# Chained sums of four selective scans on TensorE, a deferred C product on GpSimd and a later product of silu

## The chip, the cores and the metric

The kernel runs on one core of one Trainium2 chip. The metric is the device time of one execution in microseconds (us), as the median of several executions. One execution is profiled; its trace gives the views that are quoted here. The engines are called PE (TensorE's products), PEld (its weight loads), DVE (VectorE), ACT (ScalarE), POOL (GpSimd) and SP (the sync engine, which issues nearly all DMAs here).

## The reference, cut to what matters

The model is a convolution and gated selective scan block, followed by an attention and a feed-forward block on the same tokens. The scan runs over 4 batches, 4 directions, 192 channels, 16 states and 4096 positions. The part that the change touches is this:

```python
xconv = jax.nn.silu(t)                                   # t: the convolution's output
x_flat = xconv.reshape(Bn, Dn, L)                        # rows of the image
x_tr = xconv.transpose(0, 1, 3, 2).reshape(Bn, Dn, L)    # columns of the image
...                                                      # directions 0, 1; 2, 3 are these reversed
def step(h, inp):
    ut, dt, Bt, Ct = inp
    dA = jnp.exp(dt[..., None] * A[None])
    h = dA * h + (dt * ut)[..., None] * Bt[:, :, None, :]
    y = jnp.einsum('bkdn,bkn->bkd', h, Ct)
    return (h, y)
...
return y + D[None, :, :, None] * u
...
inv_y = jnp.flip(out_y[:, 2:4], axis=-1)
y = out_y[:, 0] + inv_y[:, 0] + wh_y + invwh_y           # wh_y, invwh_y: turned back to rows
mu = jnp.mean(y, axis=-1, keepdims=True)                 # a layer norm follows
```

## The kernel before

A scan is cut into 1536 pieces of 128 partitions (32 channels by 4 states) by 1024 positions: 4 batches, 4 directions in the order 1, 3, 0, 2, 4 stretches of positions, 6 groups of 32 channels, 4 sets of states. Here is the loop over pieces. `back` is a generator for all other work: the convolution of later batches, the turn of the column scans and the epilogue (layer norm, attention, feed-forward) of finished ones; the loop takes one step of it per piece.

```python
for i in range(n):
    self.at = i
    self.loads(i)                      # dl: delta and delta*u; bc: B and C rows
    if i >= 1:
        self.carry(i - 1)              # ACT, a small copy
    if i + 1 < n:
        self.decay(i + 1)              # ACT: dA = exp(dl * A)
    full = i % 8 == 3 and i > 8
    if full:
        self.evacuate(i - 4)           # ACT: ys <- yp, then stored
    elif i >= 3:
        self.reduce(i - 3)             # PE: sum over states into yp
    if i + AHEAD < n:
        self.inject(i + AHEAD)         # POOL: w = dl * B
    self.scan(i)                       # DVE: h = scan(dA, w); then w = h * C
    c.later.tick()
    ...                                # prepares delta of later pieces
    next(back, None)
    if full:
        self.reduce(i - 3)
```

The product with C goes to GpSimd or VectorE, as a static tally of their work decides, and the reduce sums over 4 sets of states in PSUM:

```python
c.vec.tensor_tensor_scan(h, dA, w, first, ALU.mult, ALU.add)
(c.gps if pool else c.vec).tensor_tensor(w, h, cr, ALU.mult)
...
for x in range(4):                     # reduce
    c.nc.tensor.matmul(
        y[32 * x : 32 * x + 32, g % 2, :], c.sum4, prod[:, 256 * x : 256 * x + 256],
        start=(q == 0), stop=(q == NQ - 1), tile_position=(0, 32 * x),
    )
```

Each direction's output `yd[k]` goes to DRAM. The turn adds directions 1 and 3 on TensorE and copies the sum in transposed order; the layer norm adds the rest, also on TensorE:

```python
for i, t in enumerate(ts):             # turn: yd[1] and yd[3]
    nc.tensor.matmul(ps, c.i96, t, start=(i == 0), stop=(i == 1))
yield
nc.scalar.copy(
    yh.rearrange("p (h w) -> p h w", w=IW)[:, :, 8 * q : 8 * q + 8],
    ps.rearrange("p (w h) -> p h w", h=IH),
)
...
for h in range(2):                     # the epilogue's layer norm
    ps = bank(f"ys{h}", h)[0:96]
    mm(ps, [(c.i96, x["y0"][:, h]), (c.i96, x["y2"][:, h]), (c.i96, x["y13"][:, h]), (c.dskip[:, h], x["u"][:, h])])
    yield
    t = f32(f"ysum{h}")
    nc.scalar.copy(t, ps)
```

silu and the sign of its input, one step (`yield`) of `back` after the other:

```python
elif s == 1:
    sg = f32("sg" + pn)[0:96, 0:128]
    nc.scalar.activation(
        sg.bitcast(F8).rearrange("p (h e i) -> p h i e", h=8, e=2),
        pz.rearrange("p (h i e) -> p h i e", h=8, e=2), AF.Sign, saturate=False,
    )
    ...
    nc.scalar.activation(e, pz, AF.Exp, scale=-1.0)
else:
    nc.scalar.activation(e, e, AF.Ln, bias=1.0)
    nc.scalar.activation(e, e, AF.Exp, scale=-1.0)
    u = f32("u" + pn)[0:96]
    c.vec.tensor_tensor(u, pz, e, ALU.mult)
```

## Time and profile before

The median is 5782.8 us over 4 executions. The profiled execution spans 5775.5 us. I cut every profile at two points of VectorE's timeline, the start of its first scan and the end of its last one:

| part | us | what sets it |
|---|---|---|
| start, to the first scan | 287.9 | loads, the convolution of batch 0, its silu |
| scans | 5321.9 | VectorE works 5026.5 of it, GpSimd 5023.6 |
| tail, after the last scan | 165.8 | last layer norm, attention, feed-forward |

VectorE thus idles 295.4 us of the middle part. The prediction below shows the lines behind this. It mentions ScalarE's waits without showing them; here they are, from the waits of ScalarE in the kernel before (what waited and its line, what it waited for, then us in total, how often, and the longest):

```profile
ACT ysum L889 <- PE ys L836: 138.9, 52, 11.0
ACT yh L746 <- PE tn L744: 44.6, 18, 10.6
```

Both instructions stand at the head of ScalarE's queue while TensorE waits for a load, and the decays stand behind them. In the kernel before, the evacuation `ys <- yp` never does this for long. Its line (count, busy us and mean ns, idle time just before and what ended it) shows 8.6 us of waiting for TensorE in all:

```profile
L1276 ACT COPY ys<-yp 128x512 f32<-128x512 f32 x192 | 111.8, 582 | 8.6 <-PE yp L1264 8.6
```

### The profile page before, as it was taken

What the parts mean: (1) busy time and instruction counts of PE and PEld (TensorE: products, weight loads), DVE (VectorE), ACT (ScalarE), POOL (GpSimd) and SP (SyncE); (2) the same over time, 40 slices, a digit from 0 to 9 for tenths busy, and PEclk for the clock granted to TensorE, in tenths of its full rate; (3) what the DMA queues carried; (4) which work ended last, traced back from release to release, by engine and by line L of the source; (5) the groups of instructions that cost most, each with busy time, mean ns of one, the idle gap of its engine ahead of it and who ended that gap; (6) DMA issues with size and microseconds to landing.
All of it is one profiled execution on the core that took longest, in us unless ns stands there. A gap on an engine that the chain in (4) does not pass through costs nothing. (4 is left out here: it accounts for less than half of the span.)

```text
span 5775.5 us, 61921 instructions
## 1 busy us (share of the span) xinstructions
PE 3419.4 (59%) x19813; PEld 1339.9 (23%) x19813; DVE 5176.7 (90%) x3422; ACT 3672.1 (64%) x5620; POOL 5080.7 (88%) x2291
## 2 busy tenths in 40 slices
PE   6446645664468755666446875563477654353577
PEld 3222222222223322222212322221122211111123
DVE  3299999999889999999999999999999999999984
ACT  5567876886556566788655656755556676554544
POOL 2099999999889999999998999999999999999980
PEclk8666755676678866666567885565688765565687
DMA  4455656655676655665567665575667555575652
GB/s 75 105 169 189 196 180 200 194 170 178 200 222 213 205 177 176 204 189 164 184 218 226 209 206 177 182 223 190 207 195 214 191 189 185 174 222 180 197 160 73
DMA packets 589452, 1069.91 MB, mean 185 GB/s; under 512 B 225867, under 2 KB 295556, under 8 KB 587332
## 3 DMA queue, kind: packets, MB, share of 16 engines
q1 hardware_dynamic: 575636, 1065.88, 59.3%
q8 instruction: 156, 2.56, 0.2%
q10 hardware_dynamic: 13488, 0.07, 0.1%
q14 instruction: 172, 1.41, 0.1%
HBM read 833.20 MB, written 229.38 MB: 184 GB/s over the span
## 5 line engine op out<-in xcount | busy, mean ns | idle before, releaser
L386 POOL TENSOR_TENSOR w<-dl,bc 128x1024 f32<-128x1024 f32 x1536 | 3578.4, 2354 | 149.2 <-PE yp L1264 73.8
L1223 ACT ACTIVATE dA<-dl,anm 128x1024 f32<-128x1024 f32 x1536 | 1714.0, 1116 | 494.6 <-DVE w L386 254.6
L1264 PE MATMUL yp<-w,sum 128*32 128x256 f32 x12288 | 1323.3, 547 | 845.8 <-ACT ys L1276 447.7
L386 DVE TENSOR_TENSOR_SCAN dA<-dA,cy,w 128x1024 f32<-128x1024 f32 x680 | 1593.1, 2343 | 109.7 <-ACT dA L1223 94.0
L386 POOL TENSOR_TENSOR w<-h,bc 128x1024 f32<-128x1024 f32 x631 | 1483.8, 2352 | 191.6 <-DVE h L386 181.0
L386 DVE TENSOR_TENSOR w<-dA,bc 128x1024 f32<-128x1024 f32 x905 | 1108.6, 1225 | 57.9 <-DVE dA L386 0.9
L386 DVE TENSOR_TENSOR_SCAN h<-dA,cy,w 128x1024 f32<-128x1024 f32 x472 | 1103.8, 2340 | 12.0 <-ACT dA L1223 10.2
L1264 PEld LDWEIGHTS yp<-w,sum 128*32 128x32 f32 x12288 | 363.1, 137 | 1941.0 <-issue 836.8
L386 DVE TENSOR_TENSOR_SCAN dA<-dA,w 128x1024 f32<-128x1024 f32 x225 | 513.6, 2283 | 38.3 <-ACT dA L1223 29.9
L1254 ACT COPY cy<-dA 128x1 f32<-128x1 f32 x680 | 105.8, 156 | 666.2 <-DVE w L386 665.7
L562 PE MATMUL cv<-tp,cw 96*96 96x512 fp8e5 x1152 | 390.8, 499 | 137.5 <-ACT r L611 110.0
L386 DVE TENSOR_TENSOR_SCAN h<-dA,w 128x1024 f32<-128x1024 f32 x159 | 362.3, 2279 | 32.0 <-POOL w L386 23.7
L562 PEld LDWEIGHTS <-cw 96*96 96x96 fp8e5 x1152 | 174.3, 158 | 358.2 <-issue 314.6
L744 PE MATMUL tn<-yt,ident 96*96 96x512 f32 x256 | 175.1, 820 | 111.8 <-DMA yt<-yd 111.1
L836 PE MATMUL ys<-ey,ident 96*96 96x512 f32 x336 | 184.7, 692 | 75.2 <-DMA ey<-yd 47.4
L1254 ACT COPY cy<-h 128x1 f32<-128x1 f32 x472 | 87.6, 186 | 193.5 <-DVE h L386 193.5
L575 ACT ACTIVATE sg<-cz 96x512 fp8e5<-96x512 f32 x64 | 159.0, 2484 | 22.1 <-DVE cz L386 22.0
L1166 ACT ACTIVATE pd<-dps,dbias,pvd 128x512 f32<-128x512 f32 x189 | 143.7, 760 | 23.1 <-PE dps L1161 23.1
L386 DVE TENSOR_TENSOR u<-cz,e 96x512 f32<-96x512 f32 x64 | 43.8, 684 | 115.6 <-ACT e L586 108.6
L1167 ACT ACTIVATE sp<-dps,dbias,pvd 128x512 f32<-128x512 f32 x189 | 144.6, 765 | 0.0
L836 PE MATMUL fc<-x,mean 96*96 96x512 f32 x54 | 51.9, 1064 | 151.9 <-DVE x L386 151.9
L386 DVE TENSOR_TENSOR pd<-dps,pu 128x512 f32<-128x512 f32 x189 | 130.7, 691 | 8.6 <-DMA pu<-ud 2.2
(305 smaller groups left out, 4448.1 us busy)
## 6 DMA issues: line engine op xcount, KB each, us to landing
dl<-dld SPq DMA_DIRECT2D x768, 512.0 KB
bc<-bcd SPq DMA_DIRECT2D x512, 512.0 KB
dld<-pd SPq DMA_DIRECT2D x126, 512.0 KB
yd<-ys SPq DMA_DIRECT2D x768, 64.0 KB
dld<-pd SPq DMA_DIRECT2D x126, 256.0 KB
yt<-yd SPq DMA_DIRECT2D x128, 192.0 KB
ey<-yd SPq DMA_DIRECT2D x58, 384.0 KB
pu<-ud SPq DMA_DIRECT2D x32, 512.0 KB
```

Source lines behind the costliest of these rows:

```text
L386: return getattr(self.eng, name)(out, *args, **kw)
L562: nc.tensor.matmul(ps, c.cw[:, j, t, 96 * h : 96 * h + 96], tpad[j][:, 8 * q + dy : 8 * q + dy + 8, dx : dx + IW], start=(j == 0 and t == ...
L575: nc.scalar.activation(sg.bitcast(F8).rearrange("p (h e i) -> p h i e", h=8, e=2), pz.rearrange("p (h i e) -> p h i e", h=8, e=2), AF.Sign ...
L744: nc.tensor.matmul(ps, c.i96, t, start=(i == 0), stop=(i == 1))
L836: self.c.nc.tensor.matmul(ps, w, x, start=(i == 0), stop=(i == len(pairs) - 1))
L1166: nc.scalar.activation(d[:, 0], ps, AF.Abs, scale=sc, bias=bi)
L1167: nc.scalar.activation(t, ps, AF.Relu, scale=sc, bias=bi)
L1223: c.nc.scalar.activation(t, self.dlt[i // NQ][0], AF.Exp, scale=c.anm[:, g, NQ * KORD[e] + q : NQ * KORD[e] + q + 1])
L1254: self.c.nc.scalar.copy(self.carries[g, q], h[:, CH - 1 : CH])
L1264: c.nc.tensor.matmul(y[32 * x : 32 * x + 32, g % 2, :], c.sum4, prod[:, 256 * x : 256 * x + 256], start=(q == 0), stop=(q == NQ - 1), tile ...
```

## The change

The intent is to take those two waits, and the TensorE and VectorE work of the sums, away. Scan 3 adds the output of scan 1 while it reduces, scan 2 adds that of scan 0, the turned sum, and D times u; the outputs are loaded into a new tile `ya` and multiplied into the PSUM tile of the reduce. Besides, the product with C on GpSimd is queued behind the next inject, sg is written in a row, silu's product comes a step later (and the taps of the convolution are spread over four steps instead of three), the turn goes ahead of the next convolution, the evacuation goes ahead of the decay, an output counts as settled after 8 pieces instead of 16, and in the last 64 pieces the work behind takes two steps per piece. The diff, cut to its core:

```diff
-                for s in range(3):
+                for s in range(4):
...
-                                sg.bitcast(F8).rearrange("p (h e i) -> p h i e", h=8, e=2),
-                                pz.rearrange("p (h i e) -> p h i e", h=8, e=2), AF.Sign, saturate=False,
+                                sg.bitcast(F8).rearrange("p (h e i) -> p h e i", h=8, e=2),
+                                pz.rearrange("p (h i e) -> p h e i", h=8, e=2), AF.Sign, saturate=False,
...
-                        else:
+                        elif s == 2:
                             nc.scalar.activation(e, e, AF.Ln, bias=1.0)
                             nc.scalar.activation(e, e, AF.Exp, scale=-1.0)
+                        else:
                             u = f32("u" + pn)[0:96]
                             c.vec.tensor_tensor(u, pz, e, ALU.mult)
... (turn: no products on TensorE, yh copied straight from the loaded yd[3])
... (layer norm: no ys products and no ysum copies; it loads the finished sum)
-        (c.gps if pool else c.vec).tensor_tensor(w, h, cr, ALU.mult)
+        if pool:
+            self.late = (w, h, cr)
+        else:
+            c.vec.tensor_tensor(w, h, cr, ALU.mult)
...
+    def load_sums(self, i):
+        b, e, ci, g, q = self.pieces[i]
+        k = KORD[e]
+        if k < 2:
+            return
+        at = CH * (NCH - 1 - ci)
+        t = c.p.ya.tile([128, 3, 256], F32, name=f"ya_{i}", tag="ya")          # one buffer
+        whole = lambda d: d.rearrange("h p l -> (h p) l")
+        srcs = [c.yd[1][b]] if k == 3 else [c.yd[0][b], whole(c.y13[b]), whole(c.ud[b])]
+        for j, src in enumerate(srcs):
+            c.nc.sync.dma_start(
+                t[:, j], src[32 * g : 32 * g + 32, at : at + CH].rearrange("d (x l) -> x d l", x=4)
+            )
+        self.sums[i // NQ] = [(t[:, j, ::-1], c.dskip[:, g] if j == 2 else c.back4) for j in range(len(srcs))]
... (reduce, on the last of the four sets of states)
+        for n, (src, w) in enumerate(more):
+            c.nc.tensor.matmul(y[:, g % 2, :], w, src, start=False, stop=(n == len(more) - 1))
... (the loop over pieces)
             self.loads(i)
+            if i % NQ == NQ - 1:
+                while KORD[self.pieces[i][1]] == 2 and self.pieces[i][0] not in c.turned:
+                    next(back)
+                self.load_sums(i)
             if i >= 1:
                 self.carry(i - 1)
+            if i % 8 == 3 and i > 8:
+                self.evacuate(i - 4)
             if i + 1 < n:
                 self.decay(i + 1)
-            full = i % 8 == 3 and i > 8
-            if full:
-                self.evacuate(i - 4)
-            elif i >= 3:
+            if i >= 3:
                 self.reduce(i - 3)
             if i + AHEAD < n:
                 self.inject(i + AHEAD)
+            self.late_product()
             self.scan(i)
...
             next(back, None)
-            if full:
-                self.reduce(i - 3)
+            if i > n - 64:
+                next(back, None)
```

## The prediction

> **What bounds the kernel now.** I read the page first, then the waits of VectorE and GpSimd alone, then busy time by stage, then the chain at the end. The kernel runs 1536 pieces of a selective scan (128x1024). Each needs one GpSimd product w<-dl,bc (the inject), one VectorE scan, and one product with C on either engine, which a static tally decides.
>
> ```profile
> PE 3419.4 (59%) x19813; PEld 1339.9 (23%) x19813; DVE 5176.7 (90%) x3422; ACT 3672.1 (64%) x5620; POOL 5080.7 (88%) x2291
> ...
> L386 POOL TENSOR_TENSOR w<-dl,bc 128x1024 f32<-128x1024 f32 x1536 | 3578.4, 2354 | 149.2 <-PE yp L1264 73.8
> ...
> L386 POOL TENSOR_TENSOR w<-h,bc 128x1024 f32<-128x1024 f32 x631 | 1483.8, 2352 | 191.6 <-DVE h L386 181.0
> L386 DVE TENSOR_TENSOR w<-dA,bc 128x1024 f32<-128x1024 f32 x905 | 1108.6, 1225 | 57.9 <-DVE dA L386 0.9
> ...
> L744 PE MATMUL tn<-yt,ident 96*96 96x512 f32 x256 | 175.1, 820 | 111.8 <-DMA yt<-yd 111.1
> L836 PE MATMUL ys<-ey,ident 96*96 96x512 f32 x336 | 184.7, 692 | 75.2 <-DMA ey<-yd 47.4
> ...
> L575 ACT ACTIVATE sg<-cz 96x512 fp8e5<-96x512 f32 x64 | 159.0, 2484 | 22.1 <-DVE cz L386 22.0
> ```
>
> Two engines are near full and nothing else is. The timeline puts the first scan at 287.85 us and the last work of the scans at about 5613. Busy time in that stretch, then in one batch's layer-norm sums, then in a stretch with hardly any work behind the scans (columns: window, length, then busy us of PE, weight loads, DVE, ACT, POOL, then clock, DMA share, GB/s):
>
> ```profile
> 287.85:5613.00 5325.15, 3159.54 (x18774) 1204.50 (x18773) 5027.10 (x3152) 3456.04 (x5310) 5026.74 (x2180) 0.67 0.61 193
> ```
> ```profile
> 1660.00:1990.00 330.00, 253.85 (x1236) 94.71 (x1234) 300.25 (x199) 195.23 (x318) 300.37 (x131) 0.82 0.69 213
> ```
> ```profile
> 5130.00:5450.00 320.00, 126.96 (x909) 42.11 (x906) 311.33 (x185) 165.52 (x252) 313.32 (x136) 0.56 0.59 190
> ```
>
> So the span is 288 us of start, 5325 of scans and 163 of tail. In the scans both engines work 5027 us: the 298 us of idle time is all that a change of waits can win there. The quiet stretch idles 2.7%, the sums 9%. What ends the idle time in the scans (VectorE, then GpSimd):
>
> ```profile
> DVE dA L386 <- ACT dA L1223: 123.9, 82, 8.5
> DVE u L386 <- ACT e L586: 44.3, 28, 3.4
> DVE h L386 <- POOL w L386: 24.0, 3, 16.8
> ```
> ```profile
> POOL w L386 <- DVE h L386: 181.0, 174, 6.0
> POOL w L386 <- PE yp L1264: 74.3, 33, 5.9
> ```
>
> VectorE waits for ScalarE's decay dA although ScalarE is only 64% busy: a decay stands in ScalarE's queue behind something that itself waits. ScalarE's own waits name it: ysum for PE's ys 138.9 us, yh for PE's tn 44.6 us. In the tail the chain goes through loads:
>
> ```profile
> 5619.26 9.52 DMA ln1b<-yd
> 5628.87 10.94 DMA eu<-ud
> 5639.91 0.81 DVE ey L386 x2
> 5641.97 3.73 PE mu L836 x4
> ```
>
> **What the Trainium skill says.** "TensorE: Matmul & The Clock Gate", section "Architectural detail: the array is 16× 32×32, not 1× 128×128", calls ScalarE, VectorE and GpSimd strict FIFOs. The trace agrees: with a third of ScalarE's time free, decays still came up to 8.5 us late. "SBUF — State Buffer", section "Door 1: The DMA port swizzle", says that consecutive accesses to one 16-byte line of SBUF run at full bandwidth and each change of line costs. The trace agrees for writes: sg writes bytes 32 apart and takes 2484 ns, while xsT, as many fp8 elements written in a row, takes 672. It agrees for reads: the ut copy reads SBUF at a 256-byte step and takes 1100 ns, while yh makes the same kind of transposition out of PSUM in 575. "DMA: Bandwidth & Descriptors", section "Anatomy of one DMA — SWDGE (gpsimd) path", says a DMA's semaphore wait happens on the issuing sequencer. Here the sync queue waited 891.8 us for decays before reloading dl, so a new load placed behind a dl load also waits.
>
> **The change, part by part.**
>
> *Chained sums.* The four directional outputs are now added inside the reduce's PSUM accumulation: scan 3 adds scan 1's output; scan 2 adds scan 0's, the turned sum, and D times u. Removed from TensorE: tn 175.1 us; ys 184.7; the D product in ys and the bias product in sy, 112 passes each like ys (184.7/336 = 0.55 us), 2 x 62; 484 us in all. Added: 96 + 288 = 384 products of 256 columns in two passes, 768 x 0.275 = 211 us. Net about -270 us, off the path. What counts is that ScalarE loses 56 ysum copies (32.5 us) with their 139 us of waits, and yh no longer waits for TensorE. yh now reads SBUF at a step, so it should cost about 1.1 us like ut: 64 x 0.52 = +34 us. Traffic is a draw: 64 x 192 KB + 96 x 384 KB leave, 384 x 128 KB come, both 50.3 MB, now in 1 KB runs instead of 2 KB.
>
> *sg written in a row.* 2484 to about 700 ns: 64 x 1.78 = -114 us of ScalarE. In the start, 16 of these lie on the chain cz, sg, e, e, e, u, v, r. One part takes 7.4 us there; without 1.8 it would take 5.6, where TensorE, busy 15 of each 20 us, also nears its limit (7.4 x 0.75 = 5.6). I take 6.0: 16 x 1.4 = **-22 us** at the start.
>
> *silu's product a step later.* u no longer stands at VectorE's head while its exponential runs: most of 44 us in the scans. In the start nothing else stands there, so no gain.
>
> *C product behind the next inject.* A GpSimd product now has one inject (2.35 us) more before it needs h. The 174 waits average 1.04 us, so most vanish as seen from GpSimd. But both engines idle the same 298 us, and GpSimd's waits are largely VectorE's lateness passed on; I count this as slack, not as a second sum.
>
> *Order and depth.* The evacuation goes ahead of the decay, the settling distance falls from 16 to 8 pieces, the turn precedes the prologue, and the work behind gets two steps per piece in the last 64 pieces. The instruction order shows no pile-up: at most 7 ScalarE instructions between two decays in both kernels. It also shows 6 instead of 4 of the last batch's eight columns done under the scans.
>
> *Sum in the scans*, by stage, with idle time (length minus VectorE's busy time, my cut of the timeline): turn and sums 1609 us, 129 idle (8.0%), to 4%: -65. Convolution 645, 50 idle (7.8%), to 4%: -25. The remaining 3070, 119 idle (3.9%), to 3.3%: -19. Against that +8 for two more columns of epilogue and +7 for waits on the added loads. **-94 us**.
>
> *Tail.* Before, mu of the last lane starts at 5642 behind 3 x 6 loads and the adds. Now two columns in two lanes need three loads each and no adds, so mu can start near 5622, and lane 0 has no second round (5672 to 5697). From mu to the end of kv took 29 us, so the middle part starts near 5653 instead of 5697: **-44 us**. The 78 us after it stay.
>
> Sum: 5783 - 22 - 94 - 44 = 5623; I say 5620.
>
> **Rivals.**
> (a) The added loads become the wait. They have one buffer, queue behind 1 MB of dl loads, and the last of them is needed by an evacuation that now stands ahead of a decay. For: DMA is already 69% busy in the sums. Against: some four pieces (14 us) lie between issue and use, and a 1.4 MB burst at the 310 GB/s seen at the start needs 4.5 us. If each of 96 loaded PSUM tiles cost 1.5 us: 5620 + 144, about 5765.
> (b) The idle time merely moves: VectorE waits for other things at ScalarE's head (fq, xq, sq wait 117 us for TensorE), or GpSimd for w buffers, because products come later. Then only start and tail count: about 5715.
> (c) The slack works everywhere and all stages reach the quiet stretch's 2.7%: 5027/0.973 = 5167, -158 in place of -94: about 5560.
>
> **Range and chances.** Start and tail are the surer 66 us; 2% is 116 us, so the scans must give 50 of their 298. (c) is as near as (b), and (a) is what would undo it. Range 5535 to 5700. Faster by over 2%: 0.78; within 2%: 0.19; slower: 0.03.
>
> **What would show it.** sg near 700 ns and yh near 1100; first scan near 266 us; u <- e gone in the scans; dA <- ACT dA from 124 to about 50; w <- h from 181 to under 60; the stretch between start and tail near 5230; tail near 119. Wrong if yp waits for the new loads by more than about 50 us and decays wait behind ys, or if POOL w <- PE yp grows beyond its 74.

## The result, and the profile after

The changed kernel takes 5711.7 us (median of 4, 5707.2 to 5716.4) against 5782.8. A ratio here is the mean time of one kernel's fast runs over that of the other's of the same rounds, so it is not quite the ratio of the medians: it is 0.988, with a 95% interval of 0.9863 to 0.9897. That is within 2%, where the prediction expected more than 2%, and above its range, which ended at 5700.

| part | before | after | change | predicted |
|---|---|---|---|---|
| start | 287.9 | 264.7 | -23.1 | -22 |
| scans | 5321.9 | 5326.6 | +4.7 | -94 |
| tail | 165.8 | 119.2 | -46.6 | -44 |

Start and tail came as worked out. The whole miss is in the scans, which gave nothing. First the page of the changed kernel: the engines' busy time, then groups (line, engine, operation and shapes, count, busy us and mean ns, idle time just before and what ended most of it):

```profile
PE 3355.5 (59%) x19813; PEld 1348.7 (24%) x19813; DVE 5157.6 (90%) x3396; ACT 3566.1 (62%) x5564; POOL 5075.9 (89%) x2295
...
L401 POOL TENSOR_TENSOR w<-h,bc 128x1024 f32<-128x1024 f32 x633 | 1490.4, 2355 | 127.7 <-DVE h L401 121.5
...
L1294 PE MATMUL yp<-ya,back 128*128 128x256 f32 x576 | 286.0, 607 | 253.9 <-DMA ya<-yd 222.7
...
L1303 ACT COPY ys<-yp 128x512 f32<-128x512 f32 x192 | 112.2, 585 | 122.9 <-PE yp L1294 112.7
```

The tn and ys products are gone, and ScalarE has 106 us less to do (3672.1 before). But the last two lines look like the old trouble again: the new products waited 222.7 us for the load of an earlier output, and the evacuation, idle for 8.6 us before, now waits 112.7 us for those products. The same stretch as the prediction's first window, from the first scan to the last (columns as there):

```profile
264.73:5591.30 5326.57, 3127.62 (x18796) 1225.91 (x18795) 5028.31 (x3161) 3392.30 (x5278) 5029.13 (x2187) 0.65 0.61 195
```

VectorE (the third number after the length) and GpSimd (the fifth) have the same work as before, in a stretch of the same length. So hardly any work was added on the bounding engines: VectorE's idle time is 298.3 us where it was 295.4. The waits of VectorE, GpSimd and TensorE in the changed kernel say what ends it now:

```profile
DVE dA L401 <- ACT dA L1221: 122.8, 70, 10.0
...
DVE u L401 <- ACT e L601: 39.8, 16, 2.5
DVE h L401 <- ACT dA L1221: 30.5, 14, 7.6
```
```profile
POOL w L401 <- DVE h L401: 121.5, 106, 4.2
...
POOL w L401 <- PE yp L1289: 74.3, 43, 6.3
```
```profile
PE yp L1294 <- DMA ya<-yd: 222.7, 78, 9.8
...
PE yp L1294 <- DMA ya<-y: 31.1, 47, 1.7
...
PE yp L1294 <- DMA ya<-ud: 26.0, 52, 1.2
```

VectorE waits for late decays 122.8 + 30.5 = 153.3 us; before it was 123.9 + 17.9 = 141.8. The prediction put the late decays down to ysum and yh; those waits are gone, and the decays are as late as before, so something else holds them now. The 39.8 us of u lie in the start, where u has nothing else to run beside. TensorE waited 222.7 + 31.1 + 26.0 = 279.8 us for the added loads.

One such event, from the changed kernel's timeline (start, length, queue or engine, operation, and in brackets the wait just before it):

```profile
1306.92 6.18 SPq L1198 DMA_DIRECT2D dl<-dld  x2
...
1313.20 0.57 SPq L1275 DMA_DIRECT2D ya<-yd  x1
...
1314.42 0.69 SPq L1275 DMA_DIRECT2D ya<-ud  x1
...
1319.61 1.22 PE L1294 MATMUL yp<-ya,back 128*128 128x256 f32 x2 [4.11 <-DMA ya<-yd]
...
1324.05 1.22 PE L1294 MATMUL yp<-ya,dskip 128*128 128x256 f32 x2 [0.88 <-DMA ya<-ud]
...
1325.30 0.58 ACT L1303 COPY ys<-yp 128x512 f32<-128x512 f32 x1 [3.68 <-PE yp L1294]
...
1325.79 1.12 ACT L1221 ACTIVATE dA<-dl,anm 128x1024 f32<-128x1024 f32 x1
...
1327.01 2.30 DVE L401 TENSOR_TENSOR_SCAN dA<-dA,w 128x1024 f32<-128x1024 f32 x1 [3.13 <-ACT dA L1221]
```

The sync queue is held 6.18 us by the two dl loads ahead (the next two, at 1325.70, take it 1.22 us; in between it waited until 1311.84 for a decay, which frees their buffer), so the first ya load leaves at 1313.20. It is used 6.4 us later, and the third one, issued at 1314.42, 9.6 us later. TensorE was ready for the first at 1319.61 - 4.11 = 1315.50, only 2.3 us after its issue. The evacuation needs all three and stands in front of the decay; the decay stands in front of the scan. VectorE loses 3.13 us. It is one event; the hold of the queue is longer than in most.

ScalarE's groups by shape show the sizes that were predicted for single instructions:

```profile
L755 ACT COPY yh<-yt 96x512 f32<-96x512 f32 x64 | 68.9, 1076 | 13.5 <-DMA yt<-yd 12.9 <-ACT sp L1165 0.5
...
L590 ACT ACTIVATE sg<-cz 96x512 fp8e5<-96x512 f32 x64 | 37.6, 588 | 25.6 <-DVE cz L401 25.4
L598 ACT ACTIVATE e<-cz 96x512 f32<-96x512 f32 x64 | 37.3, 584 | 0.0
```

sg takes 588 ns where it took 2484, now the same as its neighbour e; the prediction said 700. That e, whose own patterns did not change, took 936 ns before. yh takes 1076, as predicted. In the chain that ended last, the tail's first links are shorter than before, but the new loads head it:

```profile
5591.21 5.65 DMA ya<-ud
...
5600.93 3.62 DMA eys<-yd
5604.69 3.70 PE mu L848 x4
```

mu starts 5604.69 - 5591.30 = 13.4 us after the last scan. Before, it started 5641.97 - 5609.73 = 32.2 us after it: one load now brings a finished sum where four loads and three additions stood. From mu to the middle part (where the prediction has 5697) it was 5697.08 - 5641.97 = 55.1 us, and now 5631.82 - 5604.69 = 27.1: the second round of lane 0 is gone.

Last, the scans by direction, in the order in which they run, summed over the four batches. I counted the scan instructions of VectorE's timeline and took the starts of every 96th:

| us | scan 1 | scan 3 | scan 0 | scan 2 | last 64 pieces (in scan 2) |
|---|---|---|---|---|---|
| before | 1362 | 1308 | 1328 | 1324 | 217 |
| after | 1327 | 1309 | 1286 | 1405 | 252 |

So the change does win in the scans, 35 us in scan 1 and 42 us in scan 0. It loses 81 us in scan 2, where each PSUM tile waits for six loads (three for each of its two groups), and some 35 of these are in the last 64 pieces.

### The profile page after: what moved, and what is told of

Its sections match the earlier page's. It is cut to its first block, busy times and chain, and to the rows that moved or that the text cites.

```text
span 5710.5 us, 61945 instructions
## 1 busy us (share of the span) xinstructions
PE 3355.5 (59%) x19813; PEld 1348.7 (24%) x19813; DVE 5157.6 (90%) x3396; ACT 3566.1 (62%) x5564; POOL 5075.9 (89%) x2295
## 5 line engine op out<-in xcount | busy, mean ns | idle before, releaser
L401 POOL TENSOR_TENSOR w<-dl,bc 128x1024 f32<-128x1024 f32 x1536 | 3581.3, 2358 | 151.7 <-PE yp L1289 74.3
L1289 PE MATMUL yp<-w,sum 128*32 128x256 f32 x12288 | 1363.2, 551 | 1009.6 <-POOL w L401 580.4
L401 POOL TENSOR_TENSOR w<-h,bc 128x1024 f32<-128x1024 f32 x633 | 1490.4, 2355 | 127.7 <-DVE h L401 121.5
L401 DVE TENSOR_TENSOR_SCAN h<-dA,cy,w 128x1024 f32<-128x1024 f32 x474 | 1108.0, 2339 | 30.5 <-ACT dA L1221 30.5
L1289 PEld LDWEIGHTS yp<-w,sum 128*32 128x32 f32 x12288 | 342.4, 136 | 2080.9 <-POOL w L401 882.2
L1294 PE MATMUL yp<-ya,back 128*128 128x256 f32 x576 | 286.0, 607 | 253.9 <-DMA ya<-yd 222.7
L1294 PEld LDWEIGHTS yp<-ya,back 128*128 128x128 f32 x576 | 131.0, 274 | 423.4 <-DMA ya<-yd 281.4
L577 PEld LDWEIGHTS <-cw 96*96 96x96 fp8e5 x1152 | 161.7, 151 | 283.1 <-issue 237.0
L1303 ACT COPY ys<-yp 128x512 f32<-128x512 f32 x192 | 112.2, 585 | 122.9 <-PE yp L1294 112.7
L848 PE MATMUL yc<-eys,mean 96*96 96x512 f32 x240 | 130.5, 695 | 21.7 <-DMA esz<-szd 7.6
L401 DVE TENSOR_TENSOR dps<-dps,sp 128x512 f32<-128x512 f32 x189 | 129.1, 683 | 0.0
```

What stands on the lines that cost most here:

```text
L401: return getattr(self.eng, name)(out, *args, **kw)
L577: nc.tensor.matmul(ps, c.cw[:, j, t, 96 * h : 96 * h + 96], tpad[j][:, 8 * q + dy : 8 * q + dy + 8, dx : dx + IW], start=(j == 0 and t == ...
L848: self.c.nc.tensor.matmul(ps, w, x, start=(i == 0), stop=(i == len(pairs) - 1))
L1289: c.nc.tensor.matmul(y[32 * x : 32 * x + 32, g % 2, :], c.sum4, prod[:, 256 * x : 256 * x + 256], start=(q == 0), stop=(q == NQ - 1 and no ...
L1294: c.nc.tensor.matmul(y[:, g % 2, :], w, src, start=False, stop=(n == len(more) - 1))
L1303: c.nc.scalar.copy(t, y[:, :, ::-1] if k >= 2 else y)
```

## The experiments

My theory after the result was that the loads of ya arrive late, and pass the delay on through TensorE, the evacuation and the decay. The rivals: the place of the evacuation ahead of the decay is the cost, whatever it waits for; the added products or the added traffic slow TensorE or the DMA engines as such; the deferred C product turns GpSimd's idle time into waits for buffers. A second round asked about the doubled steps of the last 64 pieces, and whether the small parts gave what was predicted of them. All 15 kernels ran with three timed rounds; ratios are against the kernel before in the same rounds. In the tables, "scans" is always the stretch from the first scan to the end of the last, in one profile each; four executions of one kernel differ by 8 to 23 us in all (5707.2 to 5716.4 above), and the rounds ran on different chips, so a difference of some 15 us between two profiles means nothing alone.

### Without the chained sums (result wrong)

```diff
-            if i % NQ == NQ - 1:
-                while KORD[self.pieces[i][1]] == 2 and self.pieces[i][0] not in c.turned:
-                    next(back)
-                self.load_sums(i)
```

> The changed kernel without the chained loads and their products in the reduce (a wrong result on purpose: the epilogue gets scan 2's output alone); all else as in the changed kernel, 5712 us. Scans 0, 1, 2, 3 of the four batches took 331+..., in sum 1284 us (scan 0), 1327 (scan 1), 1400 (scan 2), 1312 (scan 3) there. Theory A (the gain of the removed waits is given back because loads and products of the chain hold the evacuation, and with it the decay, in scan 2): scan 2 falls from 1400 to about 1310 us, VectorE's wait for decays from 153 to under 70, time about 5620. Theory B (the loss in scan 2 comes from the doubled steps at the end and from the work that moved there, not from the chain): at most 20 us less, about 5695.

Measured: 5633.6 us, ratio 0.9758 (0.9741 to 0.9774), scans 5250.3. The output is wrong, with a relative error of 0.158, as it must be. Loads, added products and the wait for the turn are all gone; the scans get 76 us shorter. The cost is in the chained sums; which part of them, this run can't say. (The sums by direction in the expectation are off by up to 5 us from the table above.)

### The added products without their loads (result wrong)

```diff
-        t = c.p.ya.tile([128, 3, 256], F32, name=f"ya_{i}", tag="ya")
+        t = self.still                       # a resident tile of zeros
...
-        for j, src in enumerate(srcs):
-            c.nc.sync.dma_start(
-                t[:, j], src[32 * g : 32 * g + 32, at : at + CH].rearrange("d (x l) -> x d l", x=4)
-            )
```

> The chain's 384 products stay but read a tile that is resident (a wrong result on purpose), so only the 384 loads go. Theory A1 (it is the late loads that hold the evacuation): as without the chain, about 5625. Theory A2 (it is TensorE's 286 us of added products): about as the changed kernel, 5700 or more.

Measured: 5639.9 us, ratio 0.9772 (0.9758 to 0.9787), scans 5259.0; wrong by the same 0.158. TensorE still does every added product here, and only some 9 us of the scans come back against the run above. So the products themselves cost too little to tell from the noise, and 5326.6 - 5259.0 = 67.6 us are due to the loads (by the ratios, about 62). That can be their lateness or their traffic.

### The evacuation behind the decay again

```diff
-            if i % 8 == 3 and i > 8:
-                self.evacuate(i - 4)
             if i + 1 < n:
                 self.decay(i + 1)
+            if i % 8 == 3 and i > 8:
+                self.evacuate(i - 4)
```

> Only the evacuation goes back behind the decay of the next piece, as in the kernel before. Theory A with the evacuation ahead of the decay as the culprit: one decay is shielded from its wait, a decay later still has to wait behind it, and the 112.7 us that ScalarE waits there for yp fall on VectorE by about a piece (3.4 us) less each in 44 cases: about 5660. If the order of the two doesn't matter (the evacuation still stands ahead of the decay after it): 5705 to 5715.

Measured: 5686.8 us, ratio 0.9854 (0.984 to 0.9869), scans 5297.3, result correct. VectorE's wait for dA falls from 122.8 to 79.7 us. By the ratios the place is worth 0.0026 of the time, about 15 us, with intervals that just overlap, and by the scans 29; the time lies between the two forecasts. It is a place in which a late evacuation does more harm; it isn't what makes it late.

### The loads one piece earlier, ahead of the dl loads

```diff
-            if i % NQ == NQ - 1:
-                while ...
-                self.load_sums(i)
...
                 self.reduce(i - 3)
+            if i % NQ == 2:
+                while ...
+                self.load_sums(i + 1)
```

> The chain's loads are issued one piece earlier, right behind the reduce that frees their buffer and so ahead of the 1 MB of dl loads of the next piece instead of behind them. If the loads are late because they queue behind the dl loads and the decay that these wait for (theory A1): TensorE's wait for ya falls from 280 us to under 100 and the time to about 5650. If the sync queue then waits for TensorE in their place (it waited 85 us already for yp there): no gain, 5700 or more.

Measured: 5714.1 us, ratio 0.9897 (0.9879 to 0.9915), scans 5325.2, correct: no gain. The sign of theory A1 came, but not its time: TensorE's wait for ya fell from 279.8 to 53.4 us and VectorE's for dA from 122.8 to 92.5. The waits of the sync queue show where the gain went:

```profile
SPq L1275 <- PE yp L1294: 468.7, 96, 14.6
```

There is one buffer of ya. Issued this early, the load must wait until TensorE has read the buffer's last contents, and it waits at the head of the one queue that carries all loads. In the changed kernel this wait is 84.8 us. The loads behind it then come late: GpSimd waited 36.0 us for bc, against 2.7, and VectorE 12.6 us for bc and 21.5 for x1b, against 4.7 and 13.4. So an earlier load alone moves the wait from TensorE to the sync queue; it needs a free buffer too.

### Two loads for each group, in two buffers, three pieces earlier

A second buffer of three rows did not fit in SBUF when I built it. This version moves D times u to scan 3, in the turned order of u, so that scans 3 and 2 load two rows each. Bytes and number of loads stay: 96 x 2 + 96 x 2 instead of 96 x 1 + 96 x 3.

```diff
-ya=pool("yap", 1)
+ya=pool("yap", 2)
...
-        t = c.p.ya.tile([128, 3, 256], F32, name=f"ya_{i}", tag="ya")
+        t = c.p.ya.tile([128, 2, 256], F32, name=f"ya_{i}", tag="ya")
-        srcs = [c.yd[1][b]] if k == 3 else [c.yd[0][b], whole(c.y13[b]), whole(c.ud[b])]
+        srcs = [c.yd[1][b], whole(c.utd[b])] if k == 3 else [c.yd[0][b], whole(c.y13[b])]
-        self.sums[i // NQ] = [(t[:, j, ::-1], c.dskip[:, g] if j == 2 else c.back4) for j in range(len(srcs))]
+        self.sums[i // NQ] = [(t[:, j, ::-1], c.dskip[:, g] if (k, j) == (3, 1) else c.back4) for j in range(len(srcs))]
...
-            if i % NQ == NQ - 1:
+            if i % NQ == 0:
```

> The chain is kept and correct, but its loads get time: D times u joins in scan 3 (from the turned u) instead of scan 2, so that each of the two scans has two loads, the buffer shrinks from three to two rows of 256 and is doubled, and the loads are issued three pieces earlier, ahead of the dl loads, into a buffer free since the group before the last. Number of loads and bytes as in the changed kernel (ratio 0.988 to before). Theory A1 (only their lateness costs): the ratio of the run without loads, 0.977, and TensorE's wait for ya under 60 us. If the traffic or the sync queue's time costs, not the lateness: 0.985 to 0.988.

Measured: 5648.7 us, ratio 0.9781 (0.9757 to 0.9805), scans 5265.7, correct. Whether it is over 2% faster than the kernel before stays open. VectorE's wait for the decays before dA, 122.8 us in the changed kernel, is down by a third (before h, from 30.5 to 26.7):

```profile
DVE dA L401 <- ACT dA L1221: 80.4, 58, 8.5
```

TensorE no longer waits for ya at all. I paired each load of an earlier output with the first product that uses it. In the changed kernel TensorE waited for 78 of these 192 loads; in the median of these it stood ready 5.0 us after the issue, and the product began 7.5 us after it. In this run the median from issue to use is 21 us. With the same bytes, the scans are 60.9 us shorter, 90% of the 67.6 us that taking the loads away had given (by the ratios, 57 of 62). So it was mainly the lateness, not the traffic. The second buffer, the earlier issue and the even split of the loads were not tested one by one.

### The same with the evacuation behind the decay

The edit is that of the third experiment on top of the fifth.

> The same with the evacuation behind the decay as in the kernel before. If with timely loads the evacuation no longer waits, its place is worth nothing more: within 0.002 of the run with two loads each. If it still waits for the products (TensorE in order behind other work), 0.003 less.

Measured: 5646.7 us, ratio 0.977 (0.9744 to 0.9795), scans 5265.7, correct. It can't be told from the run above (0.9781). Once the loads are in time, no effect of the evacuation's place is seen.

### The C product in its old place

```diff
-        if pool:
-            self.late = (w, h, cr)
-        else:
-            c.vec.tensor_tensor(w, h, cr, ALU.mult)
+        (c.gps if pool else c.vec).tensor_tensor(w, h, cr, ALU.mult)
```

> The changed kernel with GpSimd's C product back at its place before the next inject. If the deferral hides the wait for h (the prediction's slack): GpSimd's w <- h wait goes from 121 back to about 180 us and the time grows by 20 to 40 us, ratio 0.992 to 0.995. If GpSimd's wait was VectorE's lateness passed on: within 0.002 of 0.988. If the deferral makes the reduces late and so costs: 0.984.

Measured: 5709.0 us, ratio 0.9879 (0.9854 to 0.9903), scans 5325.2, correct. The time is that of the changed kernel (0.988), but GpSimd's waits are not: 208.0 us for h instead of 121.5, and 12.0 + 6.2 for yp instead of 74.3.

### The kernel before with the deferred C product, sg in a row and silu's later product

The edit takes these three parts of the diff above, and nothing else, into the kernel before.

> The kernel before with the deferred C product, the sign written in a row and silu's product a step later, without the chained sums, the new order of the work behind and the doubled steps. The start must gain its 23 us. If the scans' waits in convolution and quiet pieces are won by these three alone: 45 us more, ratio about 0.988. If their scan part is small and the gain in scans 0 and 1 of the changed kernel comes from the chain: 0.993 to 0.996.

Measured: 5695.2 us, ratio 0.9859 (0.9837 to 0.9882), correct; first scan at 261.0, scans 5266.4, tail 165.7. Three small edits, without any chained sum, already do at least as well as the whole change (the intervals overlap): they gain 55.5 us in the scans.

### The kernel before with sg in a row alone

The edit is the swap of `"p h i e"` for `"p h e i"` on both sides.

> The kernel before with the sign alone written in a row (2484 to about 600 ns, 64 times). The three small parts together gave ratio 0.986: 26 us at the start and 56 in the scans. If this layout carries them: 0.987 to 0.989, with the start at 261 us and VectorE's wait u <- e in the scans well below 44 us without any move of the product. If it only speeds the start: 0.995.

Measured: 5727.4 us, ratio 0.992 (0.9904 to 0.9937), correct; first scan at 261.6, 26 us earlier than before; scans 5292.9, 29 shorter. The whole gain of the start is sg's. In the scans, VectorE's wait u <- e falls from 44.3 to 19.1 us by sg alone.

### The kernel before with silu's later product alone

The edit is the split into `elif s == 2` and `else`, with the taps of the convolution spread over four steps.

> The kernel before with silu's product alone moved a step behind its exponential. The prediction counted the 44 us of u <- e in the scans as won by this. If so, ratio 0.992 to 0.994 and no gain at the start. If the wait is ScalarE's backlog behind the 2.5 us sign, the product is still a little early: 0.996 to 1.0.

Measured: 5722.4 us, ratio 0.9911 (0.9896 to 0.9926), correct; first scan at 288.2, as before; scans 5261.0, 61 shorter. By direction it wins 29 us in scan 1 (1362 to 1333) and 34 in scan 0 (1328 to 1294). So this part and sg overlap: 61 and 29 alone, 55.5 together with the third part. Of the 61, VectorE's idle time gives 46 (295.4 to 249.6) and its busy time 15 (5026.5 to 5011.4), of which 12 lie in three products m (15.8 us before, 4.2 here); why these are shorter is open. The spread of the taps is a part of this edit, and no run separates it.

### The kernel before with the deferred C product alone

> The kernel before with GpSimd's C product alone behind the next inject. Undoing it in the changed kernel changed nothing (0.988 both), while its wait for h went from 121 to 208 us and its wait for TensorE's yp from 74 to 12. If it swaps one wait for the other: ratio 0.998 to 1.002, w <- h down from 181 to about 80, w <- yp up from 74 to about 150. If it is worth something where the reduces aren't late: 0.993 to 0.996.

Measured: 5770.5 us, ratio 0.9994 (0.9979 to 1.0009), correct. The waits of GpSimd in this run:

```profile
POOL w L386 <- PE yp L1274: 158.1, 70, 7.2
...
POOL w L386 <- DVE h L386: 78.1, 79, 3.8
```

Before it was 74.3 for yp and 181.0 for h. The sum is nearly the same, 236 against 255, and the time is the same. Deferring the product makes GpSimd wait less for h, and more for a free w buffer, because each product, and so the reduce that frees its buffer, comes later (TensorE's wait for GpSimd's w before a reduce rises from 356.2 to 440.8 us).

### Two loads in two buffers, and no doubled steps

The changed kernel's last 64 pieces take 252 us, the kernel before's 217, and even with the loads in time (two loads, two buffers) they take 247. The waits of VectorE in the changed kernel from 5345 us to the end of the scans, about the last 64 pieces, begin so:

```profile
DVE g L401 <- PE sy L848: 14.7, 7, 4.6
DVE vks L401 <- PE vk L848: 6.7, 4, 2.3
```

Neither is a scan. Both belong to the work behind. A chain such as sy, then g, is cut into steps so that one piece lies between the product on TensorE and its use on VectorE. With two steps per piece both fall into one piece, and VectorE waits at its head. This run takes the second step away:

```diff
-            if i > n - 64:
-                next(back, None)
```

The norm then runs into the switch to the tail's mode half way, so the mode is also fixed at its start (`alone = self.alone`).

> The run with two loads in each scan (ratio 0.978), with one step of the work behind per piece to the end instead of two in the last 64 pieces (and the last batch's mode fixed when a column begins, without which this does not build). The doubled steps cost the last 64 pieces 247 - 218 = 30 us. If the two more columns under the scans are worth more than that in the tail (44 us predicted): slower, 0.980 to 0.981. If the tail would be as short without them: faster, 0.973.

Measured: 5620.0 us, ratio 0.9729 (0.9714 to 0.9744), scans 5232.6, tail 128.9, correct. The last 64 pieces take 216 us and VectorE's waits for sy and vk there are gone. With the last run below it is the fastest correct kernel. Against the three small edits without chained sums its scans are 33.8 us shorter and its tail 36.8: that is about what the chained sums and the new order bring once the loads are in time. Its window over the scans:

```profile
260.72:5493.33 5232.61, 3077.06 (x18743) 1226.38 (x18743) 5023.99 (x3157) 3386.00 (x5267) 5027.83 (x2186) 0.66 0.62 198
```

VectorE's work is the same 5024 us; the idle time is 209 us instead of 298.

### No doubled steps alone

The edit is the same, on the changed kernel.

> The changed kernel (0.988) with one step of the work behind per piece to the end, its late loads kept. If the doubled steps cost 30 us in the last 64 pieces and give 10 in the tail as in the pair of runs with two loads each: 28 us less (0.005), ratio 0.983. If the cost of the last pieces was the late loads after all: 0.988 or more.

Measured: 5693.8 us, ratio 0.9857 (0.9838 to 0.9876), scans 5305.6, tail 130.4, correct. The doubled steps cost 21 us in the scans and win 11 in the tail. In the last 64 pieces alone, where they act, they cost 32 us (251.5 to 219.1).

### No loads and no doubled steps (result wrong)

> Neither the chain's loads (a wrong result on purpose) nor the doubled steps. If the two losses add up: ratio 0.977 less 0.005, 0.972, and a stretch of scans near 5228 us where the prediction has 5322 - 94 = 5228. If they overlap: 0.975 or more.

Measured: 5619.9 us, ratio 0.974 (0.9715 to 0.9766), scans 5223.0, tail 127.1; wrong by 0.158. The four runs make a square:

| scans, us | doubled steps | single steps |
|---|---|---|
| loads as in the change | 5326.6 | 5305.6 |
| no loads | 5259.0 | 5223.0 |

The loads cost 67.6 or 82.6 us, the doubled steps 21.0 or 36.0, and both together 103.6. The 15 us between these are not clear of the noise: scan 1, which has no added loads, differs by 13 of them. In scans 3 and 2, which alone have them, the loads cost 61.4 or 62.4 us and the doubled steps 27.0 or 28.0. The ratio, 0.974, lies between the two forecasts, and its interval holds both. In scan 2 alone it is 1405, 1378, 1352 and 1322 us: without both, the 1324 of the kernel before.

### The fastest version with the C product in its old place

> The fastest version so far (two loads in each scan, single steps, 0.973) with GpSimd's C product at its old place. If the deferral only swaps waits: 0.972 to 0.975. If it pays where the reduces are in time: 0.976 or more.

Measured: 5620.1 us, ratio 0.9732 (0.9712 to 0.9752), scans 5230.3, correct. GpSimd waits 134.7 us for h. With the loads in time and single steps, the deferred product is still worth nothing.

## Why the prediction was wrong, and where it was right

**The step that failed: "+7 for waits on the added loads".** It should have been some 62 us (61.4 and 62.4 in the scans that have the loads, 68 and 83 over the whole stretch). The prediction had the mechanism as its rival (a), to the last link ("the last of them is needed by an evacuation that now stands ahead of a decay"), and set it aside with "some four pieces (14 us) lie between issue and use". The 14 us are the distance in the program. Where TensorE waited, the medians are these: the load was issued 2.3 us after VectorE had begun the scan of that piece, TensorE stood ready 5.0 us after the issue, and the product began 7.5 us after the issue, not the 4.5 us of a 1.4 MB burst. The prediction quoted the waits of the sync queue (891.8 us) and did not ask when it would reach the new load. How much of the lateness is the queue being held, as for 6.18 us in the event above, is open: the pair of dl loads took it a median of 2.4 us before the loads that were waited for, and 1.9 us before the others. The prediction's own test, "wrong if yp waits for the new loads by more than about 50 us and decays wait behind ys", came true: 280 us and 112.7. Of rival (a)'s 144 us, somewhat under half was measured.

**The step that was missing: the doubled steps.** The prediction named the "two steps per piece in the last 64 pieces", checked that ScalarE's instructions do not pile up, and gave them no cost beside the two columns' 8 us. By the last 64 pieces of three pairs of runs they cost 32, 31 and 32 us there (21 to 36 over the whole scans), in waits at VectorE's head between steps that no longer have a piece between them. Of the 47 us that the tail won, some 10 are theirs (119.2 against 130.4, 127.1 and 128.9).

**What remained was right in size.** Without both costs the scans take 5223.0 us, where the prediction's sum makes 5321.9 - 94 = 5228, and the time is 5619.9 where it said 5620. That closeness is partly luck: the -94 already held 15 us for the loads and the two columns, without which it would be -109 and 5213, and this kernel's tail is 127.1 us, not the predicted 119. Whether the gain fell on the stages as forecast was not checked; by direction it lies in scans 1 and 0 (46 and 45 us), and 55.5 us came without any chained sum.

**Start: right.** sg 588 ns (predicted 700) and -23 us (predicted -22; -21 to -27 in all runs with this start). The run with sg alone shows that it is sg, and the run with silu alone that silu's part gives the start nothing.

**silu's later product: the right place, too small.** "Most of 44 us" turned out as 61 alone. The wait for e in the scans is gone, and VectorE's idle time is down by 46 us. That fit is partly luck, since its wait for decays fell by 29 us and others rose. The other 15 us are busy time, which nobody forecast. Since the three small parts give 55.5 us together, the stages' sums of the prediction, which never said which part wins what, could not have been split by part.

**Deferred C product: right for the time, wrong for the sign to look for.** It was counted as no gain, and three pairs of runs agree (0.9994; 0.9879 against 0.988; 0.9732 against 0.9729). But w <- h did not fall under 60: it was 121.5 in the changed kernel and 78.1 alone, and waits for w buffers rose in its stead, as rival (b) had it. That POOL w <- PE yp stayed at 74.3 in the changed kernel hides two effects: with the product in its old place it is 12.0.

**TensorE: wrong, and without consequence.** The added products took 286.0 us and, for those with D, 93.8, together 380, where the prediction had 211 from half an ys pass each: a pass of 256 columns took 286.0/576 = 0.50 us, nearly the 0.55 of one of 512; why, no run here tells. It stayed off the path: all products without their loads cost some 9 us, within the noise.

**Tail: right** at -46.6, and in both of its places: 18.8 us before mu (predicted 20), and 28.0 after it, where the second round is gone (predicted 24).

## What to carry to other kernels

A load's slack is not the distance in the program. It is the time from the moment at which its queue really issues it to the moment at which the engine is ready for it, less the load's own time under that traffic. The trace of the kernel before shows how far the queue and the engines are apart. If an operand can be late, give it a second buffer and an earlier issue before it becomes the head of three queues in a row; here both together were worth 61 us, while an earlier issue (by one piece) into a single buffer was worth nothing. And steps that are cut so that other work lies between them should not be taken two at a time unless the chain within them has something else to hide behind; here that cost 32 us in 64 pieces.

## What the Trainium skill lacked or had wrong

- "DMA: Bandwidth & Descriptors", section "Anatomy of one DMA — SWDGE (gpsimd) path", gives a DMA as about 2.0 us plus its bytes over 436 GB/s, which makes an estimate of 2.3 us for 128 KB. The loads here come from the sync queue and not from GpSimd, and the page has no figure for a small load that is issued behind 1 MB of others: in the timeline it was 6.4 to 9.6 us from issue to use, and 5.65 us in the tail, where little else moved.
- "SBUF — State Buffer", section "Door 1: The DMA port swizzle", has the line rule that this confirms (sg 2484 to 588 ns; yh 577 out of PSUM, 1076 out of SBUF). Its remark that a non-contiguous pattern in PSUM is slow speaks of matmuls only. ScalarE reading every second float32 of PSUM lost nothing: sg 588 ns, and e, which reads the same tile in a row, 584. Neither did yh in the kernel before, at a 256-byte step of PSUM: 577 ns, and ysum, in a row, 581.
- "TensorE: Matmul & The Clock Gate", section "Architectural detail: the array is 16× 32×32, not 1× 128×128", calls ScalarE and VectorE strict FIFOs and TensorE's queue a partial reorder window that can pull weight loads ahead of products. The section has no word on what a product that waits for a DMA does to the queues behind it. Here 280 us of such waits on TensorE came out as 113 us at ScalarE's evacuations, and mending them shortened the scans by 61 us.
